# Attention scores for maxima and for exponentials: one ring of four PSUM banks in place of two and two

## The chip, the cores and the metric

The kernel runs on one core of a Trainium2 chip. The metric is the device time of one execution in microseconds (us). A core has engines with instruction queues of their own: TensorE (PE in the profile, with its weight loads as PEld), VectorE (DVE), ScalarE (ACT), GpSimd (POOL) and SyncE (SP), which here only issues transfers. Each queue is worked off in its order; an instruction that waits holds up those behind it on its engine. A matmul writes into PSUM, of which a core has eight banks of 128 partitions by 512 float32 numbers; DVE and ACT read the result from there, and the bank can be written again once it has been read.

## The reference, cut to what matters

The input x has 4 sequences of 512 tokens with 128 features. Four layers follow one another, each added to x after a layer norm: a block with a state-space scan (Mamba) and a mixture of experts, a feed-forward layer, an attention layer, and the same feed-forward layer again. The change is in the attention.

```python
x = x + _L0_attn_a_ref(_layernorm(x), ...)       # scan over 512 tokens, then 8 experts, top 2
x = x + _L0_ffn_ref(_layernorm(x), ...)
x = x + _L0_attn_b_ref(_layernorm(x), ...)       # attention, 16 heads of 8 features
x = x + _L0_ffn_ref(_layernorm(x), ...)
...
q_lat = jnp.einsum('bqhd,hdl->bhql', q, k_eff)
attn = jnp.einsum('bhql,bkl->bhqk', q_lat, c_kv) / sqrt(hs)
attn = jnp.where(causal, attn, -jnp.inf)
attn = jax.nn.softmax(attn, axis=-1)
y_lat = jnp.einsum('bhqk,bkl->bhql', attn, c_kv)
```

The weights of the attention are scaled so that scores are large: the softmax must subtract each row's maximum.

## The kernel before

The first part of the kernel (its last scan step begins at 356.6 us) is the scan, in which the order of the instructions on each engine is written out by hand (`manual_schedule`). The experts, the feed-forward layers and the attention of a sequence follow as soon as its data are there. In the attention's part, from line 1114 on, the order on each engine is not that of the text: a scheduler takes at each step the earliest instruction of the text that could run by its own estimate, and a PSUM or SBUF tile is given a free buffer at that moment. The order that comes out is fixed when the kernel is built; on the chip each engine follows it and waits on semaphores.

The attention works in units: a unit `u` is half the heads (8) of one sequence, so there are 8 units, 0 to 7. For each unit:

- `fill(u)` loads the queries and keys of the unit into the stacks `qs` and `ks` (three of each, taken in turn) from the DRAM tensors `q_d` and `k_d`, with transfers that SP issues. `project(b)` has written these for sequence `b`: layer norm on DVE, `axn` on ACT, transposes and the matmuls `pq` and `pu` on PE, a split into three bfloat16 parts on ACT and POOL, and a transfer to DRAM.
- `maxima(u)` computes all scores with queries on the partitions, 22 bank-sized tiles `sc` a unit: matmuls at line 1186, the causal mask added by a matmul at line 1190, and then a DVE reduction to the row's maximum (`mx`, lines 1182 and 1199). The maxima are split into parts, transposed (`pmx`, line 1209), copied by ACT (`mT`) and written by three transfers that ACT issues (line 1215) into three further rows of `qs`. With them a second matmul of queries and keys yields scores from which the maximum is already subtracted.
- `exps(G)` computes the scores again, with keys on the partitions, for a group `G` of four heads (two groups to a unit, 16 in all): 10 tiles `st` a group, matmuls at line 1238, mask at line 1246, and an ACT exponential of the bank into a tile `p` (line 1251). There are 12 buffers for `p` (`PBUFS`).
- `weigh(G)` multiplies the 10 `p` tiles of a group by the values (`po`, 32 matmul records at line 1265, given a high priority), copies the sum by ACT (`ayT`), transposes it (`pyt`), copies it (`yt`), divides by the sums on DVE and, after the fourth group of a sequence, adds the result to x. The last feed-forward layer of that sequence follows.

The text runs a step of `exps(G)`, one or two steps of `maxima(u + 1)` and a step of `weigh(G - 1)` in turn, and beside them the feed-forward layers and projections of later sequences (`streams`).

Of the eight PSUM banks one is `ps_m` (transposes, projections, `pmx`, `pyt`), two are `ps_s` (feed-forward and experts), one is `ps_o` (`po`). The other four are the subject here:

```python
ps_q, ps_t = pool("ps_q", 2, space=PSUM), pool("ps_t", 2, space=PSUM)   # line 1124
sc = ps_q.tile([P, L], F32, tag="sq", name="sc")                        # line 1183, maxima
pt = ps_t.tile([P, L], F32, tag="st", name="st")                        # line 1234, exps
```

The pools have `reuse_waits="tile"`: the first matmul into a buffer waits for the tile that had the buffer before it, and for no other.

Of the kernel before, what the change touches and what calls it, by code (L numbers as in the profile page):

```python
# [8 lines left out]
F32 = mybir.dt.float32  # L9
# [5 lines left out]
PSUM = bass.MemoryType.PSUM  # L15

P = 128
B, L, C = 4, 512, 128
# [19 lines left out]
def block_kernel(ctx, tc, x, rms1_w, rms2_w, in_proj_w, conv_w, conv_b, x_proj_w,  # L38
# [1075 lines left out]
    with ExitStack() as second:  # L1114
        def pool(name, bufs, **more):
            return second.enter_context(
                tc.tile_pool(name=name, bufs=bufs, reuse_waits="tile", **more)
            )
# [2 lines left out]
        dram = second.enter_context(  # L1121
            tc.tile_pool(name="a_dram", bufs=2, space=bass.MemoryType.DRAM)
        )
        ps_q, ps_t = pool("ps_q", 2, space=PSUM), pool("ps_t", 2, space=PSUM)
        ps_o = pool("ps_o", 1, space=PSUM)


# [93 lines left out]
        def exps(G):  # L1221


            u, h0 = G // 2, 4 * (G % 2)
            q, k = qs[u % 3], ks[u % 3]
            probs[G] = got = [{} for _ in range(4)]

            for blocks in (
                [(0, 0, 0)], [(1, 0, 0)], [(2, 0, 0)], [(3, 0, 0)],
                [(0, 1, 0), (0, 3, L - P)], [(1, 1, 0), (1, 3, L - P)],  # L1230
                [(2, 1, 0), (2, 3, L - P)], [(3, 1, 0), (3, 3, L - P)],
                [(0, 2, 0), (1, 2, 2 * P)], [(2, 2, 0), (3, 2, 2 * P)],
            ):
                pt = ps_t.tile([P, L], F32, tag="st", name="st")
                p = w2.tile([P, L], F32, tag="p", name="p", bufs=PBUFS)
                for j, kt, c in blocks:
                    rows = slice(kt * P, (kt + 1) * P)
                    nc.tensor.matmul(  # L1238
                        pt[:, c : c + L - kt * P], k[:, h0 + j, rows],
                        q[:, h0 + j, kt * P : L],  # L1240
                        start=(c == 0), stop=False, skip_group_check=True,
                    )
                    got[j][kt] = p[:, c : c + L - kt * P]

                n, step = len(blocks), blocks[-1][2] // P or 1
                nc.tensor.matmul(  # L1246
                    pt.rearrange("p (a c) -> p a c", c=P)[:, 0 : step * (n - 1) + 1 : step, :],
                    identb, maskk.unsqueeze(1).to_broadcast([P, n, P]),
                    start=False, stop=True, skip_group_check=True,
                )  # L1250
                ready[G] = nc.scalar.activation(p, pt, AF.Exp, scale=scale).ins  # L1251
                yield
# [82 lines left out]
        for G in range(2 * UNITS + 1):  # L1335
            u = G // 2
            if G % 2 == 0:
# [6 lines left out]
                while u + 1 < UNITS and filled <= u + 1:  # L1344
                    turn(*streams)
                    if filled // 2 in stores:
                        fill(filled)
                        filled += 1
                more = maxima(u + 1) if u + 1 < UNITS else iter(())
            scores = exps(G) if G < 2 * UNITS else iter(())  # L1350
            weighed = weigh(G - 1) if 1 <= G else iter(())
            for step in range(10):
# [74 lines left out]
```

## Time and profile before

| what | value |
|---|---|
| time, median of 3 runs | 882.34 us (880.51 to 889.71) |
| the profiled execution's own time | 900.44 us |
| its span (first to last instruction) | 898.7 us |
| mean granted TensorE clock | 0.904 |
| PE, DVE, ACT, POOL busy | 723.7, 569.0, 409.5, 308.2 us |
| first and last matmul of the maxima (line 1186) | 473.6 and 833.8 us |
| first and last matmul of the exponentials (line 1238) | 523.9 and 871.7 us |
| DVE reductions of maxima, lines 1182 and 1199 | 168 and 8 |
| ACT exponentials, line 1251 | 160, mean 601 ns |

A group of instructions is shown with its source line, engine and operation, the tile written and those read, the count, the busy time and the mean of one, and then how long the engine stood idle before these instructions and what ended most of that. A row of a time stretch gives the busy time of PE, weight loads, DVE, ACT and POOL, the granted clock and the share of the DMA engines. A row of the waits gives who waited for whom: total in us, number of times, longest. The profiled execution was 2.1% longer than the median of the runs.

### The profile page before, as it was taken

What the parts mean: (1) busy time and instruction counts of PE and PEld (TensorE: products, weight loads), DVE (VectorE), ACT (ScalarE), POOL (GpSimd) and SP (SyncE); (2) the same over time, 40 slices, a digit from 0 to 9 for tenths busy, and PEclk for the clock granted to TensorE, in tenths of its full rate; (3) what the DMA queues carried; (4) which work ended last, traced back from release to release, by engine and by line L of the source; (5) the groups of instructions that cost most, each with busy time, mean ns of one, the idle gap of its engine ahead of it and who ended that gap; (6) DMA issues with size and microseconds to landing.
All of it is one profiled execution on the core that took longest, in us unless ns stands there. A gap on an engine that the chain in (4) does not pass through costs nothing.

```text
span 898.7 us, 12363 instructions
## 1 busy us (share of the span) xinstructions
PE 723.7 (81%) x3957; PEld 439.7 (49%) x3967; DVE 569.0 (63%) x1165; ACT 409.5 (46%) x796; POOL 308.2 (34%) x234
## 2 busy tenths in 40 slices
PE   8988797689698986777837789989667897599887
PEld 5633242233276751574724567856433453255445
DVE  4799999889988999563417753337643277166324
ACT  3848655737843541242410245444146533544652
POOL 1155765775675367673122003000331301200000
PEclk9998798879989997888977999999869899889999
DMA  5157221221466644263544437853200310300000
GB/s 134 38 208 284 69 60 42 72 66 49 133 204 193 195 149 119 83 190 124 181 132 135 151 95 218 231 150 113 83 24 1 109 45 3 113 30 13 2 13 12
DMA packets 83258, 95.85 MB, mean 107 GB/s; under 512 B 9841, under 2 KB 56121, under 8 KB 82041
## 3 DMA queue, kind: packets, MB, share of 16 engines
q1 hardware_dynamic: 78681, 87.09, 31.4%
q0 software_dynamic: 2944, 7.34, 2.4%
q10 hardware_dynamic: 1568, 0.63, 0.3%
q8 instruction: 32, 0.52, 0.2%
q14 instruction: 33, 0.27, 0.1%
HBM read 76.47 MB, written 18.28 MB: 105 GB/s over the span
## 4 chain that ended last, share of the span: by engine, by line
PE 28%; DMA 8%; DVE 7%; ACT 6%; issue 5%; POOL 3%; another core or an unknown queue 1%; SPq 1%; ACTq 0%; POOLq 0%; DVEq 0%
PE po L1265 4%; DMA ks<-k_d 4%; PE mpg L380 3%; PE mpd L392 3%; PE mpu L380 3%; ACT p L1251 3%; PE sc L1186 2%; DVE mx L1182 2%; PE pg L451 2%; PE pu L453 2%; PE st L1238 2%; PE fpd L478 2%; DMA wgu<-in_Wg_dram 2%; DMA k_d<-parts 2%
## 5 line engine op out<-in xcount | busy, mean ns | idle before, releaser
L953 POOL TENSOR_TENSOR hc<-hst,cs 128x1024 f32<-128x1024 f32 x63 | 148.3, 2354 | 111.6 <-issue 24.6
L894 PE MATMUL yp<-hc,ident 128*128 128x512 f32 x256 | 145.7, 698 | 41.0 <-POOL hc L953 39.2
L939 DVE TENSOR_TENSOR_SCAN hst<-da,bx 128x1024 f32<-128x1024 f32 x64 | 146.3, 2287 | 9.2 <-POOL hc L953 1.7
L1182 DVE TENSOR_REDUCE mx<-sc 128x1 f32<-128x384 f32 (+3 forms) x168 | 101.8, 635 | 67.6 <-PE sc L1190 66.2
L1251 ACT ACTIVATE p<-st 128x512 f32<-128x512 f32 x160 | 90.6, 601 | 51.5 <-PE st L1246 28.5
L894 PEld LDWEIGHTS yp<-hc,ident 128*128 128x128 f32 x256 | 52.1, 217 | 121.3 <-POOL hc L953 78.7
L1186 PE MATMUL sc<-ks,qs 125*128 125x128 bf16 (+3 forms) x256 | 68.5, 325 | 40.3 <-DMA ks<-k_d 17.6
L874 ACT ACTIVATE da<-delta,A 128x512 f32<-128x512 f32 (+1 forms) x128 | 84.8, 714 | 34.8 <-DVE hst L939 30.0
L323 DVE SCALAR_TENSOR_TENSOR thm<-thm,mpg 128x512 f32<-128x512 f32 x53 | 36.1, 681 | 73.2 <-ACT thm L386 72.5
L916 DVE TENSOR_TENSOR bx<-du,pb 128x1024 f32<-128x1024 f32 x64 | 78.3, 1223 | 6.6 <-PE pb L884 4.7
L415 POOL DMA_INDIRECT yk<-yg,rows_y x32 | 32.3, 1009 | 126.0 <-DMA yg<-ym 82.3
L1238 PE MATMUL st<-qs,ks 128*128 128x384 bf16 (+3 forms) x246 | 58.5, 307 | 20.7 <-ACT p L1251 12.0
L380 PE MATMUL mpg<-xTm,wgu 128*128 128x128 f32 x424 | 64.8, 291 | 6.7 <-DVE thm L323 3.1
L380 PEld LDWEIGHTS mpg<-xTm,wgu 128*128 128x128 f32 x424 | 57.6, 204 | 18.3 <-issue 8.5
L392 PE MATMUL mpd<-wd,mh 128*128 128x128 f32 x424 | 60.2, 286 | 6.0 <-ACT xTm L373 4.3
L380 PE MATMUL mpu<-xTm,wgu 128*128 128x128 f32 x424 | 59.7, 284 | 1.5 <-DVE mh L324 1.4
L392 PEld LDWEIGHTS mpd<-wd,mh 128*128 128x128 f32 x424 | 53.8, 198 | 11.0 <-ACT xTm L373 7.3
L386 ACT ACTIVATE thm<-mpg 128x512 f32<-128x512 f32 x53 | 31.7, 598 | 56.7 <-DVE base L408 32.5
L380 PEld LDWEIGHTS mpu<-xTm,wgu 128*128 128x128 f32 x424 | 54.9, 201 | 2.0 <-DVE mh L324 1.6
L373 ACT ACTIVATE xTm<-mpt,r2w 128x128 f32<-128x128 f32 x53 | 19.4, 366 | 63.2 <-PE mpt L371 55.3
L396 ACT COPY ym<-mpd 128x128 f32<-128x128 f32 x53 | 14.1, 267 | 72.3 <-PE mpd L392 46.0
L1186 PEld LDWEIGHTS <-qs 125*128 125x128 bf16 x256 | 25.4, 106 | 43.7 <-issue 36.0
(261 smaller groups left out, 1202.7 us busy)
## 6 DMA issues: line engine op xcount, KB each, us to landing
cs<-c_d SPq DMA_DIRECT2D x64, 256.0 KB
wgu<-in_Wg_dram SPq DMA_DIRECT2D x53, 256.0 KB
wgu<-in_Wu_dram SPq DMA_DIRECT2D x53, 256.0 KB
wd<-in_Wd_dram SPq DMA_DIRECT2D x53, 256.0 KB
xg<-zero SPq DMA_DIRECT2D x8, 1024.0 KB
qs<-q_d SPq DMA_DIRECT2D x24, 192.0 KB
ks<-k_d SPq DMA_DIRECT2D x24, 192.0 KB
xt<-xg SPq DMA_DIRECT2D x53, 64.0 KB
```

The source lines that it names most:

```text
L323: nc.vector.scalar_tensor_tensor(th, th, 1.0, g, ALU.add, ALU.mult)
L380: nc.tensor.matmul(pp[:, f, :], w[:, k, f * P : (f + 1) * P], rows_in, start=True, stop=True,)
L392: nc.tensor.matmul(pd, hT[:, f, :], w[:, f, :], start=(f == 0), stop=(f == NFC - 1))
L874: nc.scalar.activation(da[:, e, e:], delta[b][:, e, e:], AF.Exp, scale=A[:, e, n : n + 1])
L894: nc.tensor.matmul(yps[b][:, e, :], ident, hc[:, e, :], start=(n == 0), stop=(n == NS - 1))
L916: nc.vector.tensor_tensor(bxs[s], du[s // NS], taps[s][1].unsqueeze(1).to_broadcast([P, NE, L]), ALU.mult)
L939: nc.vector.tensor_tensor_scan(hst.rearrange("p e l -> p (e l)"), dec.pop(s).rearrange("p e l -> p (e l)"), bxs.pop(s).rearrange("p e l -> ...
L953: done = (nc.vector if end else nc.gpsimd).tensor_tensor(hc, hst, cs.unsqueeze(1).to_broadcast([P, NE, L]), ALU.mult).ins
L1182: nc.vector.tensor_reduce(*taken, AX.X, ALU.max)
L1186: nc.tensor.matmul(sc[:, c : c + w], q[0:MXR, h, t * P : w], k[0:MXR, h, 0:w], start=(h == h0), stop=False, skip_group_check=True,)
L1238: nc.tensor.matmul(pt[:, c : c + L - kt * P], k[:, h0 + j, rows], q[:, h0 + j, kt * P : L], start=(c == 0), stop=False, skip_group_check=True,
L1251: ready[G] = nc.scalar.activation(p, pt, AF.Exp, scale=scale).ins
```

## The change

The two pools become one of four banks, and the tiles `st` take the tag of the tiles `sc`. Both kinds of score tile then draw from the same four banks: a tile of either kind takes the next one that is free. No instruction of work is added or removed.

```diff
@@ -1121,7 +1121,8 @@
-        ps_q, ps_t = pool("ps_q", 2, space=PSUM), pool("ps_t", 2, space=PSUM)
+
+        ps_q = ps_t = pool("ps_q", 4, space=PSUM)
         ps_o = pool("ps_o", 1, space=PSUM)
@@ -1231,7 +1232,7 @@
-                pt = ps_t.tile([P, L], F32, tag="st", name="st")
+                pt = ps_t.tile([P, L], F32, tag="sq", name="st")
                 p = w2.tile([P, L], F32, tag="p", name="p", bufs=PBUFS)
```

## The prediction

> **What bounds the kernel now.** The change touches nothing ahead of the first maxima at 473.6 us, so I read the attention's part alone: first the busy time of each engine in stretches, then the waits of PE for its score banks, then the queues of PE, DVE and ACT in order of time where such waits lie. The stretches:
>
> ```profile
> core 0: us, PE busy (x) PEld busy (x) DVE busy (x) ACT busy (x) POOL busy (x), PEclk, DMA share, GB/s
> ...
> 722.00:740.00 18.00, 17.73 (x112) 11.25 (x115) 15.68 (x27) 7.76 (x14) 1.00 (x1) 0.96 0.08 30
> 740.00:758.00 18.00, 14.21 (x97) 7.22 (x90) 16.60 (x50) 3.64 (x8) 0.28 (x1) 0.91 0.01 2
> 758.00:786.00 28.00, 16.56 (x112) 8.31 (x111) 5.13 (x30) 17.47 (x35) 8.70 (x9) 0.86 0.30 90
> 786.00:836.00 50.00, 47.42 (x346) 27.22 (x352) 33.48 (x72) 24.29 (x43) 2.54 (x2) 0.91 0.06 20
> 836.00:877.00 41.00, 34.19 (x264) 17.54 (x256) 7.90 (x27) 24.34 (x48) 1.27 (x1) 0.96 0.03 8
> ```
>
> From 722 to 740 and from 786 to 836 PE is the bound (17.7 of 18, 47.4 of 50 us). From 740 to 758 it is DVE (16.6 of 18): the maxima of unit 5, and between their reductions the layer norm of the last sequence's projection. From 758 to 786 no engine is: the kernel waits for that projection's way through POOL and DRAM (queries and keys of unit 6 land at about 785). From 836 to 877 PE and ACT take turns on the last groups. Before 653 the experts share PE, and from 653 to 722 the end is set by the third sequence's chain of gathers, feed-forward, projection and transfers. The waits for a bank, over 470 to 898 us:
>
> ```profile
> PE st L1238 <- ACT p L1251: 12.0, 16, 3.4
> PE sc L1186 <- DVE mx L1182: 10.7, 38, 0.8
> ```
>
> That is 22.7 us in 54 waits, all that more banks could remove.
>
> **What the change removes.** With four banks behind either kind, a kind that is alone can have four tiles open, not two. PE then gets ahead by two tiles more, once; after that it goes at the reader's pace again. So a run of waits shrinks by two reader steps at most, and only if the reader itself wasn't the bound.
>
> Maxima alone, 740 to 758. PE (time, us, line, idle before) and below it DVE:
>
> ```profile
> 754.48 0.38 PE L1186 MATMUL sc<-ks,qs 125*128 125x512 bf16 x1 [0.25 <-DVE mx L1182]
> ...
> 756.91 0.38 PE L1186 MATMUL sc<-ks,qs 125*128 125x512 bf16 x1 [0.18 <-DVE mx L1182]
> 757.12 0.22 PE L1190 MATMUL sc<-maskq,identb 128*128 128x128 bf16 x1
> 757.18 1.07 PE L539 MATMUL pq<-axT,w_qk 128*128 128x512 f32 x2
> ```
>
> ```profile
> 753.73 3.72 DVE L1182 TENSOR_REDUCE mx<-sc 128x1 f32<-128x512 f32 x6 [0.27 <-PE sc L1190]
> ```
>
> Six reductions stand without a gap in 3.72 us, 0.61 each: DVE sets the pace, and the maxima end when they ended. But `pq`, a step of the last projection, stands behind five such `sc` tiles; its input `axT` was there at 754.2 (ACT 753.62 plus 0.59), and it began at 757.18. Two tiles of lead take 2 x 0.61 = **1.2 us** from it, and `pq` lies on the way to unit 6's keys, for which PE stands idle before 786. This counts in full.
>
> Beside each other, 786 to 836. PE is the bound; 1.2 us of `sc` waits (5 times) lie in it and no `st` wait. At most **1.2 us** go.
>
> Exponentials alone, 836 to 877. PE waits 4.4 us for ACT there, the longest one first (PE), then what ACT did (ACT), then the end of the stretch (ACT, PE):
>
> ```profile
> 844.65 0.38 PE L1238 MATMUL st<-qs,ks 128*128 128x256 bf16 x2 [1.96 <-ACT p L1251]
> ```
>
> ```profile
> 844.00 1.09 ACT L1251 ACTIVATE p<-st 128x512 f32<-128x512 f32 x2 [1.85 <-DMA qs<-mT]
> ...
> 868.41 4.28 ACT L1251 ACTIVATE p<-st 128x512 f32<-128x512 f32 x7
> ```
>
> ```profile
> 872.75 2.36 PE L1265 MATMUL po<-p,va 128*32 128x512 f32 x32 [0.69 <-ACT p L1251]
> ```
>
> At 844 ACT had been issuing the three `mT` transfers (1.96 us from 841.70) and then worked without a gap to the `po` at 847.4, which needs its last exponential: PE's 1.96 us there are covered by ACT, and the gain is nothing. At the end ACT does seven exponentials in 4.28 us, 0.61 each, and the last `po` waits for them. Just before, ACT stood idle for 2.01 and 1.87 us (before `ayT` at 864.04 and `fo` at 866.50) while PE did `po` and `fpd`. The buffers `p` come free with that `po`, at about 864; with two more tiles ready in PSUM, ACT does two exponentials during `fpd`: 2 x 0.61 = **1.2 us** less at the end.
>
> Elsewhere: in 473 to 487 the maxima of unit 0 are paced by DVE (11.9 of 14 us busy, and what is missing is the start): nothing. In 653 to 722 the longest `st` wait (3.4 us at 663.35) has the transpose of `xn` behind it, but `xn` came from ACT at 663.24 to 664.9, late by DVE's layer norm: nothing. Waits before 653 lie beside the experts' transfers: nothing.
>
> Sum of what goes: 1.2 + 1.2 + 1.2 = **3.6 us**.
>
> **What it adds.** No instruction is new. New are two waits: an `sc` tile can now stand behind an exponential, an `st` tile behind a reduction. A group may hold its banks for longer: exponentials run two tiles into the next group (12 `p` buffers, 10 used) and then wait for `po`. Today those that wait hold two banks, with the change up to four, and after `po` a maxima tile must wait for ACT's first exponential, 0.60 us by its row. Behind that `sc` on PE stands whatever follows: feed-forward matmuls, the next `st`. From below: nothing, if the tile behind `po` is not an `sc`, or a bank is free. From above: 0.6 us at each of the two `po` inside the stretch bound by PE (804.70, 816.99), 1.2 us. I take the middle, **+0.6**, since of the two one is followed by an `sc` straight after its mask (807.06), the other by the value matmuls.
>
> The order on the engines is made anew. In the stretches where PE is the bound it picks by place in the text, as today; I give it nothing, and keep plus or minus 6 us for the range: five 0.6 us tiles ahead of `pq` today, as many more or fewer, at two such places.
>
> Sum: -3.6 + 0.6 = **-3.0 us** of the profiled 900.44 us, 0.33%. The runs' median is 0.98 of the profiled time, so -2.9 from 882.34: **879.4 us**.
>
> **Two rules against the rows.** The Trainium skill (Perfetto Trace Analysis, Optimization Strategy) reads the same gap repeating on the engine that should be saturated as a sign that PSUM may have too few buffers. The gaps of 0.16 to 0.25 us ahead of each `sc` are just that. By the rule all 22.7 us would be for the taking, 860 us. Against it speaks another sentence of the skill (TensorE: Matmul & The Clock Gate, HAM oscillation): in a kernel made contiguous, double-buffering PSUM "gave no further gain", which here would mean 882. The row decides: DVE's six reductions without a gap say that the pace isn't PE's, and leave only what stands behind the queue, 3.0 us.
>
> **Rivals.** (1) *Every bank wait from 722 us on counts.* There the end is set by PE or by what stands in its queue: 2.8 + 0.7 (740 to 758) + 2.6 + 1.2 + 4.4 = 11.7 us, and 0.9 of `po` waits: -12.6, scaled **870**. For it: PE is the busiest engine. Against: two of the five terms are covered by DVE or ACT, as shown. (2) *Exponentials that wait for `p` hold all four banks.* The maxima then stand for `po` (2.36 us, as today) and for four exponentials more, 4 x 0.58 = 2.3 us. Four such `po` from 786 to 836 (786.30, 804.70, 816.99, 835.79) cost 9.2 us, two before (712.98, 739.78) 4.6; unit 7's maxima have a slack of 4.0 us (split ready at 836.24, `pmx` on PE at 840.32). Sum +9.8, **892**. It decides from the second such `po` on, when the slack is used up. For it: `st` of a step comes before `sc` in the text. Against: from 743 to 757 the maxima run a unit ahead of the exponentials, so few wait when groups change. (3) *The banks go round in the order of the text.* Then unit 5's maxima couldn't fill the 14 us from 743 to 757 in which unit 4's exponentials aren't allowed yet: up to +14, **896**. Against: PE's queue isn't in the order of the text even now. (4) *Nothing moves*: wherever both kinds run, PE is the bound, and the order stays: **882**.
>
> **Numbers.** My forecast 0.42 (its own range 872 to 888), rival 1 0.20, rival 2 0.22, rival 3 0.08, rival 4 0.08. Faster or slower by 1% (8.8 us, about what a measurement of this kernel can tell from no change): faster is rival 1 and a little of mine, 0.22; slower is rivals 2 and 3 and the order's upper end, 0.31; within 1% the rest, 0.47. The range: 866 to 900 leaves out the lower end of rival 1 and the upper ends of 2 and 3.
>
> **What would show it.** Right: `st` waits for ACT fall from 12.0 to under 7 us and `sc` waits for DVE stay above 6, since DVE paces them; ACT's last run of exponentials is five, not seven; `pq` of the last sequence begins nearer to its `axT` than 3 us. Rival 2: PE waits of `sc` for `p` of over 1 us behind each `po`, DVE idle longer before `mx`. Rival 3: no run of 22 `sc` without an `st`. Wrong altogether: a shift of over 6 us in when the last keys land (785) that comes from the order on POOL, ACT or SP and not from a bank.

## The result: 0.8% slower, and the profile after

| kernel | median | runs |
|---|---|---|
| before | 886.12 us (880.51 to 892.18) | 20 |
| after | 892.14 us (886.73 to 899.48) | 20 |

The ratio is 1.0079, 95% interval [1.0054, 1.0104]. The forecast was 0.33% less, so it had the wrong sign; the time lies in the range. The profiled execution of the kernel after took 892.26 us, close to its median, with a span of 890.5 us and a clock of 0.902. (From line 1125 on its line numbers are one higher than before.)

The waits for a score bank did go. These are the waits of the kernel after (engine, line, waited for, us in total, times, longest), over 460 to 898 us; the first line is not a bank's and is read below:

```profile
PE pt L178 <- ACT xn L167: 19.3, 4, 16.9
...
PE st L1239 <- DVE mx L1183: 1.9, 3, 1.1
PE st L1239 <- ACT p L1252: 1.8, 7, 0.5
...
PE sc L1187 <- ACT p L1252: 1.2, 3, 0.7
...
PE sc L1187 <- DVE mx L1183: 0.9, 5, 0.2
```

In place of 22.7 us in 54 waits there are 5.8 us in 18, and the kernel is slower all the same. New is the first line: one wait of 16.9 us for `xn`, the input of a feed-forward layer. To see where it stands, the stretches of the kernel after (busy us of PE, weight loads, DVE, ACT, POOL; granted clock; DMA share; GB/s):

```profile
600.00:653.00 53.00, 32.34 (x278) 24.63 (x275) 23.89 (x64) 16.90 (x35) 13.24 (x14) 0.83 0.32 94
653.00:690.00 37.00, 31.61 (x220) 18.35 (x220) 26.05 (x103) 20.68 (x40) 4.67 (x5) 0.92 0.02 6
...
740.00:758.00 18.00, 13.68 (x77) 6.89 (x77) 4.64 (x23) 7.84 (x16) 2.92 (x3) 0.72 0.01 2
758.00:786.00 28.00, 23.68 (x174) 12.62 (x173) 15.53 (x49) 16.07 (x31) 5.71 (x6) 0.87 0.30 96
786.00:836.00 50.00, 45.51 (x355) 27.57 (x356) 32.14 (x73) 25.83 (x47) 2.53 (x2) 0.94 0.06 17
```

The execution of the kernel before that the prediction used was 14 us over its own median. For the comparison I take the control of the first experiment instead: the kernel before with its own order written down (ratio to before 1.0005). Its two first stretches:

```profile
600.00:653.00 53.00, 41.22 (x273) 27.91 (x272) 32.10 (x86) 16.93 (x36) 16.25 (x17) 0.81 0.25 76
653.00:690.00 37.00, 29.68 (x172) 14.53 (x171) 12.79 (x73) 21.91 (x44) 9.09 (x10) 0.90 0.12 34
```

From 600 to 653 PE does 32.3 us of work where it did 41.2, and DVE 23.9 where it did 32.1. The work has moved into the next stretch: DVE 26.1 us there in place of 12.8. The tiles say which work it is. The 22 maxima tiles of unit 3 were reduced from 604.9 to 642.1 us in the control; in the kernel after they are reduced from 657.7 to 683.4. The first and the last line of these reductions, in the control and then in the kernel after:

```profile
604.91 1.28 DVE L1182 TENSOR_REDUCE mx<-sc 128x4 f32<-128x512 f32 x2
...
641.43 0.68 DVE L1199 TENSOR_REDUCE mx<-sc 128x1 f32<-128x512 f32 x1
```

```profile
657.65 2.58 DVE L1183 TENSOR_REDUCE mx<-sc 128x4 f32<-128x512 f32 x4
...
682.70 0.69 DVE L1200 TENSOR_REDUCE mx<-sc 128x1 f32<-128x512 f32 x1
```

**Why they moved.** PE's queue holds 176 maxima tiles (m) and 160 exponential tiles (E). Their order from the start of the attention, before and after:

```
before  m x44  E x24  mm EE mm E m E m E m E m E mmm EE m E m E mm E m ...  m x25  E x30 ...
after   m x22  E m E mm E m E mm ... E m  E x6  m E mm E m E mm ... (so to the end)
```

After is the order of the text: one exponential, then one or two maxima, and six exponentials where a unit ends. In both orders no tile stands ahead of an earlier one of its own tag. Two tiles of one tag are handed out by this scheduler in the order in which the text asks for them, so a tile can't be given a bank ahead of one that stands before it in the text. With two tags that held inside each kind, and the maxima could run a whole unit ahead of exponentials that weren't due yet. With one tag it holds across both kinds. The sentence in the description of the kernel that a tile is given a free buffer when its instruction is taken is true between tags only. The change thus did two things: it made four banks of two and two, and it tied the two kinds' order.

### The profile page after: what moved, and what is told of

The parts are those of the page before. It is cut to its first block, busy times and chain, and to the rows that moved or that the text cites. A ratio compares the mean times of both kernels' runs of the same rounds, so it can differ in the third digit from the quotient of the medians.

```text
span 890.5 us, 12376 instructions
## 1 busy us (share of the span) xinstructions
PE 712.7 (80%) x3967; PEld 443.8 (50%) x3967; DVE 569.2 (64%) x1165; ACT 411.3 (46%) x796; POOL 307.4 (35%) x234
## 3 DMA queue, kind: packets, MB, share of 16 engines
q1 hardware_dynamic: 78681, 87.09, 32.1%
## 5 line engine op out<-in xcount | busy, mean ns | idle before, releaser
L953 POOL TENSOR_TENSOR hc<-hst,cs 128x1024 f32<-128x1024 f32 x63 | 149.0, 2366 | 110.3 <-issue 23.5
L894 PE MATMUL yp<-hc,ident 128*128 128x512 f32 x256 | 143.2, 687 | 42.5 <-POOL hc L953 40.4
L1183 DVE TENSOR_REDUCE mx<-sc 128x1 f32<-128x384 f32 (+3 forms) x168 | 98.6, 634 | 87.7 <-PE sc L1191 87.4
L1187 PE MATMUL sc<-ks,qs 125*128 125x128 bf16 (+3 forms) x256 | 66.5, 330 | 24.7 <-DMA ks<-k_d 14.3
L380 PE MATMUL mpg<-xTm,wgu 128*128 128x128 f32 x424 | 65.5, 295 | 14.6 <-DVE thm L323 7.3
L1239 PE MATMUL st<-qs,ks 128*128 128x512 bf16 (+3 forms) x256 | 62.8, 312 | 7.7 <-DMA qs<-mT 3.6
L380 PE MATMUL mpu<-xTm,wgu 128*128 128x128 f32 x424 | 62.1, 291 | 0.0
L380 PEld LDWEIGHTS mpu<-xTm,wgu 128*128 128x128 f32 x424 | 57.5, 208 | 0.0
L1191 PE MATMUL sc<-maskq,identb 128*128 128x128 bf16 (+2 forms) x176 | 47.4, 269 | 0.0
```

Of the source, the lines that this page charges most:

```text
L380: nc.tensor.matmul(pp[:, f, :], w[:, k, f * P : (f + 1) * P], rows_in, start=True, stop=True,)
L894: nc.tensor.matmul(yps[b][:, e, :], ident, hc[:, e, :], start=(n == 0), stop=(n == NS - 1))
L953: done = (nc.vector if end else nc.gpsimd).tensor_tensor(hc, hst, cs.unsqueeze(1).to_broadcast([P, NE, L]), ALU.mult).ins
L1183: nc.vector.tensor_reduce(*taken, AX.X, ALU.max)
L1187: nc.tensor.matmul(sc[:, c : c + w], q[0:MXR, h, t * P : w], k[0:MXR, h, 0:w], start=(h == h0), stop=False, skip_group_check=True,)
L1191: nc.tensor.matmul(sc[:, 0 : n * w].rearrange("p (h k) -> p h k", k=w)[:, :, t * P : w], identb, maskq.unsqueeze(1).to_broadcast([P, n, P] ...
```

## The experiments

Every kernel was compared with runs of the kernel before on the same chip. One table of stretches serves them all, in us of one profiled execution each: from the first reduction of the maxima on DVE to the first gather of the experts' rows for sequences 2 and 3 (a), to the feed-forward layer's first transpose for sequence 2 (b), to project's store of `k_d` for sequence 2 (c), the same for sequence 3 (d), and to the end of the span (e). The ratio is that of all its runs to before.

| kernel | a | b | c | d | e | ratio and interval |
|---|---|---|---|---|---|---|
| two_old_order | 165.5 | 19.3 | 39.4 | 66.1 | 129.7 | 1.0005 [0.9983, 1.0027] |
| two_new_order | 170.1 | 18.0 | 50.7 | 66.0 | 130.2 | 1.0127 [1.0089, 1.0166] |
| after | 171.9 | 18.1 | 48.6 | 63.6 | 124.4 | 1.0079 [1.0054, 1.0104] |
| lock_early | 172.5 | 18.1 | 47.7 | 65.5 | 128.1 | 1.0174 [1.0132, 1.0215] |
| lock_late | 168.1 | 19.2 | 39.1 | 61.8 | 127.2 | 0.9918 [0.9879, 0.9957] |
| lock_unit2 | 165.7 | 18.1 | 46.3 | 64.1 | 129.6 | 1.0034 [1.0016, 1.0052] |
| lock_units01 | 171.6 | 21.5 | 37.6 | 63.2 | 128.3 | 1.0104 [1.0067, 1.0142] |
| lock_units013 | 171.0 | 21.6 | 39.0 | 68.6 | 128.2 | 1.0049 [1.0028, 1.0069] |
| four_late | 166.6 | 19.2 | 39.2 | 60.5 | 124.5 | 0.9874 [0.9821, 0.9927] |
| four_ahead | 160.6 | 26.3 | 41.7 | 81.1 | 119.5 | 1.0158 [1.0122, 1.0194] |
| ahead_012 | 164.5 | 29.1 | 44.2 | 58.9 | 123.0 | 0.9969 [0.9951, 0.9987] |
| ahead_02 | 168.7 | 26.0 | 41.8 | 59.3 | 124.3 | 0.9925 [0.9902, 0.9949] |
| ahead_2 | 168.7 | 23.5 | 41.8 | 58.9 | 122.8 | 0.9946 [0.9923, 0.9970] |

One execution strays by some us from its median, so the table shows where a kernel loses; how much it loses is read from the ratio. How far a stretch strays is seen from the first profile of the kernel before, the same program as two_old_order: it has 165.2, 24.1, 39.1, 65.7 and 130.0 us. Between these two b differs by 4.8 us, the others by 0.4 at most.

### Order or banks

Two kernels keep two banks for each kind. One has the queues of PE, DVE, ACT and SP tied to the order of the kernel before, the other to that of the kernel after (POOL's order is the same in both). The edit, for both:

```diff
+ORDERS = {
...
+def in_order(tc, names, engines):
...
+        for a, b in zip(row, row[1:]):
+            tc.add_manual_dep(b, a.name, order, reason="the order written down")
...
         block_kernel(tc, *args)
+        in_order(tc, ORDERS, ('PE', 'DVE', 'Activation', 'SP'))
```

two_old_order, the control:

> The kernel before, with each engine's queue (PE, DVE, ACT, SP) written down in the order that it has anyway. Any theory: the same program, ratio 1.000 within 0.3%. It gives a second profile of the kernel before, whose first one was 14 us longer than its median: I expect a span near 885 us, the first maxima at 460 to 466 us.

two_new_order:

> Two banks for each kind as before, but each engine's queue (PE, DVE, ACT, SP) in the order of the changed kernel, in which score tiles follow the text: no maxima tile ahead of an exponential's tile that stands before it in the text. Theory A (the order is the cost, the banks themselves give a little back): slower than before by 0.8 to 1.3%, 893 to 898 us, at or above the changed kernel's 892. Theory B (the shared banks cost, by tiles that hold a bank the other kind needs; the order is neutral): 884 to 888 us, ratio 0.998 to 1.002.

Measured: 1.0005 and 1.0127. The order alone, with no bank changed, makes the kernel slower by 1.3%; writing an order down costs nothing. In the table the loss stands in a (4.6 us) and c (11.3 us). In a the experts' last matmul comes 166.4 us after the first reduction of maxima where it came after 161.6; why it does I haven't traced, and what follows explains c. What the banks give back is after against two_new_order, the same queues with four banks: 1.0079 against 1.0127, about 0.5% or 4 us, though the two intervals overlap. In the profiles most of it lies in e, 130.2 against 124.4 us, and there the table divides by the banks: the eight profiles with two banks for each kind at the end have 127.2 to 130.2 us, that of the kernel before among them, the six with four have 119.5 to 124.5. The reverse, four banks in the old order, can't be had: inside one tag the old order isn't possible. It wasn't tried.

### Early units or late ones

Here only the first matmul of each score tile is tied to the one before it in the text, in chosen units; all other instructions are ordered by the scheduler as before.

```diff
+        def in_text_order(ins, where):
+            if not (where < 4):            # lock_early; lock_late: where >= 4
+                tied.clear()
+                return
+            if tied:
+                tc.add_manual_dep(ins, tied[0].name, order, reason="score tiles in the order of the text")
+            tied[:] = [ins]
...
+                        if h == h0:
+                            in_text_order(ins, u - 1)                 # maxima(u)
...
+                    if (j, kt, c) == blocks[0]:
+                        in_text_order(ins, u)                         # exps, unit u
```

> Two banks for each kind as before; score tiles are tied to the order of the text for the exponentials of units 0 to 3 and the maxima of units 1 to 4, and free after that. Theory A, with the loss where the two first profiles show it (first maxima to the third sequence's keys in DRAM, 229 us before and 240 after): slower by 0.8 to 1.5%, 893 to 899 us. If the loss lies in the later units: within 0.3% of before. Theory B: within 0.3% of before.

> Two banks for each kind as before; score tiles are tied to the order of the text only for the exponentials of units 4 to 7 and the maxima of units 5 to 7. Theory A, with the profiles read as above (196 us from there to the end before, 188 after): faster than before by 0.4 to 0.9%, 878 to 883 us. If the loss lies in the later units: slower by 0.8 to 1.5%. Theory B: within 0.3% of before.

Measured: 1.0174, more than the 0.8 to 1.5% expected, and 0.9918. Together they make 0.9%, by the intervals no contradiction to the 1.3% of the whole order. The same tie loses in the first half and gains in the second: the order isn't bad in itself, its place decides. The late gain can be read line by line in the layer norm of the last sequence's projection. In two_old_order these are the input `x`, the norm's first and last step on DVE, the transposed result `axT`, the last `sc` tile ahead of `pq`, and `pq` itself, for which the norm is wanted:

```profile
723.09 1.27 POOL L484 TENSOR_TENSOR x<-base,fo 128x512 f32<-128x512 f32 x1 [19.89 <-ACT fo L483]
...
724.40 0.87 DVE L153 BATCH_NORM_STATS2 st<-x 128x6 f32<-128x128 f32 x4 [0.46 <-POOL x L484]
...
732.06 0.15 DVE L162 SCALAR_TENSOR_TENSOR nm<-mv,rs_r 128x4 f32<-128x4 f32 x1
...
737.72 0.59 ACT L182 COPY axT<-pt 128x512 f32<-128x512 f32 x1 [3.50 <-PE pt L178]
...
741.05 0.38 PE L1186 MATMUL sc<-ks,qs 125*128 125x512 bf16 x1 [0.19 <-DVE mx L1182]
...
741.32 1.07 PE L539 MATMUL pq<-axT,w_qk 128*128 128x512 f32 x2
```

In lock_late, where no `sc` stands ahead of `pq`:

```profile
725.07 1.27 POOL L484 TENSOR_TENSOR x<-base,fo 128x512 f32<-128x512 f32 x1 [19.76 <-ACT fo L483]
...
726.38 0.87 DVE L153 BATCH_NORM_STATS2 st<-x 128x6 f32<-128x128 f32 x4 [0.46 <-POOL x L484]
...
730.65 0.16 DVE L162 SCALAR_TENSOR_TENSOR nm<-mv,rs_r 128x4 f32<-128x4 f32 x1
...
733.47 0.58 ACT L182 COPY axT<-pt 128x512 f32<-128x512 f32 x1 [0.52 <-PE pt L178]
...
734.11 1.22 PE L539 MATMUL pq<-axT,w_qk 128*128 128x512 f32 x1 [0.77 <-ACT axT L182]
```

From the start of `x` to `pq` it is 18.2 us in the one and 9.0 in the other. The norm takes 7.8 us from first to last step where unit 5's reductions stand between its steps, 4.4 where they don't; then the transposes and `pq` stand between and behind the `sc` tiles of unit 5 on PE, or don't: from the norm's last step to `pq` it is 9.3 us in the one and 3.5 in the other. In the early half the exchange goes the other way. In two_old_order the norm of sequence 2's projection runs from 666.47 to 670.96, 4.5 us, since unit 3's maxima are long done; in the kernel after they stand between its steps, and it takes 7.6. First and last step in two_old_order, then the kernel after:

```profile
666.47 0.87 DVE L153 BATCH_NORM_STATS2 st<-x 128x6 f32<-128x128 f32 x4 [4.61 <-POOL x L484]
...
670.83 0.13 DVE L162 SCALAR_TENSOR_TENSOR nm<-mv,rs_r 128x4 f32<-128x4 f32 x1
```

```profile
677.65 0.87 DVE L153 BATCH_NORM_STATS2 st<-x 128x6 f32<-128x128 f32 x4 [0.65 <-POOL x L484]
...
678.72 0.66 DVE L1183 TENSOR_REDUCE mx<-sc 128x1 f32<-128x512 f32 x1
679.29 0.16 DVE L428 TENSOR_SCALAR ln_v<-mv 128x4 f32<-128x4 f32 x1
679.36 0.68 DVE L1183 TENSOR_REDUCE mx<-sc 128x1 f32<-128x512 f32 x1
...
679.96 0.16 DVE L136 TENSOR_SCALAR rs_t<-ln_v 128x4 int32<-128x4 int32 x1
...
685.10 0.14 DVE L162 SCALAR_TENSOR_TENSOR nm<-mv,rs_r 128x4 f32<-128x4 f32 x1
```

In the rows from 679.29 to 682.63 each small step (0.16 us) waits for a reduction of 0.68. These 3.1 us are a third of the 9.2 by which stretch c grew; another 4.6 lie ahead of it, in the feed-forward layer, which shares PE with the same maxima: from its first transpose to `x` it takes 22.4 us (653.90 to 676.34) against 17.8 (647.37 to 665.17). And while these maxima could have run (the last transfer of their queries and keys was issued at 590.3 us), PE stood idle, since the transpose of `xn` is next in its queue (kernel after, PE; in two_new_order, with two banks for each kind, the same wait takes 17.5 us):

```profile
635.06 1.93 PE L1146 MATMUL pv<-veff,qk 64*128 64x128 f32 x8 [0.66 <-ACT mT L1214]
653.90 0.47 PE L178 MATMUL pt<-ident,xn 128*128 128x128 f32 x1 [16.91 <-ACT xn L167]
```

### Which early unit

The same tie as above, with other conditions:

```diff
-            if not (where < 4):
+            if not (where == 2):           # lock_unit2
+            if not (where < 2):            # lock_units01
+            if not (where in (0, 1, 3)):   # lock_units013
```

> Two banks for each kind, as before; only the score tiles of unit 2's exponentials and unit 3's maxima are tied to the order of the text, so that the 22 tiles of unit 3's maxima no longer run in one piece ahead of unit 2's exponentials. Theory A (most of the early loss is that unit 3's maxima move from the stretch at 605 to 641 us, where PE waits for the experts and the gathers, to a place beside ffn and project of sequence 2): the way from the transposes of ffn's xn to project's store of k for sequence 2 grows by 7 to 10 us over the 39.4 us of the two banks with their own order, and the time is 0.7 to 1.2% above before, 891 to 895 us. Rival C (the loss is spread over the early units alike, since each tied tile waits for its neighbour): about a quarter of the 1.7% of the four tied units, 0.4%, 888 to 889 us. Rival D (the loss comes from the end of the experts, which units 0 and 1 delay): within 0.3% of before.

> Two banks for each kind; tied are only the exponentials of units 0 and 1 and the maxima of units 1 and 2. Theory A: the first gathers of the experts' rows come 4 to 8 us later than the 628 us of the two banks with their own order, unit 3's maxima stay ahead of the gathers, the way through ffn and project of sequence 2 keeps its 39 to 41 us, and the time is 0.3 to 0.8% above before, 888 to 892 us. Rival C (spread alike): two quarters of 1.7%, 0.8 to 0.9%, 892 to 893 us. Rival D (all of the loss sits here): 1.4 to 1.7%, 897 to 900 us.

> Two banks for each kind; tied to the order of the text are the score tiles of lock_early (exponentials of units 0 to 3, maxima of units 1 to 4) without those of unit 2's exponentials and unit 3's maxima. Theory G (unit 2's tie is dear when its neighbours are tied too: with four banks its release alone took the time from 1.0079 to 0.9946): most of lock_early's 1.7% goes, 1.003 to 1.008 of before. Theory H (the shares of the units add up: 1.74% less lock_unit2's 0.34%): 1.012 to 1.016.

Measured: 1.0034, 1.0104 and 1.0049. Lock_unit2 stretches c by 6.9 us to 46.3, nearly what theory A expected, but the time rises by 0.3% only, as rival C said; in its profile 1.2 us come back in b and 2.0 in d. Lock_units01 delays the gathers by 6 us, as A expected, and costs 1.0%, more than A's 0.3 to 0.8% and again nearest to C. So by these two the loss seemed spread alike. But then lock_units013, three of the four units, should cost some 1.3%; it costs 0.5% and fits theory G: without unit 2's tie most of lock_early's 1.7% is gone, and c is back at 39.0 us. So unit 2's tie is worth 1.25% beside the others and 0.3% by itself. The parts don't add up, and one pair is odd: lock_units013 ties more than lock_units01 and costs no more, by intervals that just touch. How the early loss divides among the units stays open; that it is an early loss, and that taking unit 2's tie away recovers most of it, does not.

### Four banks without the early loss

First, two and two banks up to unit 3, and four from there:

```diff
-        ps_q, ps_t = pool("ps_q", 2, space=PSUM), pool("ps_t", 2, space=PSUM)
+        ps_q, ps_t, tag = scores_from("ps_q", 2), scores_from("ps_t", 2), "st"
...
             u = G // 2
+            if G == 8:
+                banks.close()
+                ps_q = ps_t = scores_from("ps_qt", 4)
+                tag = "sq"
```

> Two banks for each kind up to unit 3's exponentials and unit 4's maxima, and from there on four banks that both kinds take in turn. Theory A (order and banks add up: the late order alone measured 0.9918, and the banks gave back 0.5% where the order was held): 0.986 to 0.992 of before, 873 to 878 us; the waits of late score tiles for a bank fall under 2 us. Rival E (the banks' gain came in the early units, or goes when the pools are exchanged in mid-course, where the new tiles wait for all old ones): 0.992 to 0.998, 878 to 883 us.

Measured: 0.9874, as theory A had it. It is faster than both kernels (876.6 us against 883.87 of before on that chip), and 0.4% better than lock_late, with overlapping intervals again. The two share the order of the score tiles, but not of everything: some transposes, feed-forward matmuls and exponentials stand elsewhere in the queues of PE, DVE and ACT. As in the pair after and two_new_order, e is where the banks show, 127.2 against 124.5 us. The bank waits of late tiles (710 to 876 us) are 1.2 us, all of `st` for ACT, so under 2 as expected; but lock_late had only 2.3 there, 1.2 of `st` and 1.1 of `sc`. What went is 1.1 us, less than the 4 us between the two ratios.

Then the other way, with one tag throughout: if the text sets the order, change the text.

```diff
                 more = maxima(u + 1) if u + 1 < UNITS else iter(())
+                for _ in range(22 if u < 4 else 0):        # four_ahead
+                    next(more)
```

> Four banks in turn, as in the changed kernel, but the text has all 22 tiles of the next unit's maxima ahead of the exponentials of units 0 to 3, and from unit 4 on it is the changed kernel's text. Theory A (the loss is the order that one tag forces, and the text sets that order): unit 3's maxima run again before the gathers, at 600 to 645 us, the way through ffn and project of sequence 2 falls from the changed kernel's 49 us to 39 to 43, and the time is 0.985 to 0.995 of before, 872 to 880 us. Rival F (sharing the banks itself costs in the early units, whatever the order, for instance because maxima that wait for the fill hold a bank that exponentials would have had): still 1.002 to 1.010 of before, 887 to 894 us.

Measured: 1.0158, far from theory A's number and past rival F's as well. Unit 3's maxima do run before the gathers, and stretches a, c and e are good; b is 7 us longer than in the control, and most of the loss is in d, 81.1 us. Its cause stands in one line of PE (four_ahead):

```profile
683.28 2.07 PE L549 MATMUL pu<-qk,w_up 64*128 64x512 f32 x2 [1.16 <-ACT full L553]
708.37 0.58 PE L1187 MATMUL sc<-ks,qs 125*128 125x128 bf16 x4 [23.03 <-DMA ks<-k_d]
```

My edit had put unit 4's maxima ahead of unit 3's exponentials too. Unit 4 is the first of sequence 2, whose keys were only being stored; with one tag the exponentials, ready all the time, stand behind them, and PE has nothing for 23.0 us. So the next runs leave that unit out:

```diff
-                for _ in range(22 if u < 4 else 0):
+                for _ in range(22 if u < 3 else 0):        # ahead_012
+                for _ in range(22 if u in (0, 2) else 0):  # ahead_02
+                for _ in range(22 if u == 2 else 0):       # ahead_2
```

> Four banks in turn; the text has all 22 tiles of the next unit's maxima ahead of the exponentials of units 0, 1 and 2 (four_ahead without unit 3). Theory A2 (four_ahead lost because unit 3's exponentials stood behind unit 4's maxima, which waited 23.0 us for sequence 2's stored k): that wait goes, and the stretch from project's store of k for sequence 2 to that of sequence 3 falls from 81 us to 63 to 68; the time falls by 10 to 15 us from four_ahead's, to 0.995 to 1.005 of before, and if nothing else is out of place to 0.985 to 0.995. Rival F (sharing the banks costs in the early units whatever the order): 1.005 to 1.012.

> Four banks in turn; the maxima of units 1 and 3 stand whole ahead of the exponentials of units 0 and 2, those of the other units as in the changed kernel. It is the text that comes nearest to the order in which the kernel before runs its score tiles up to unit 3. Theory A2: first gathers 165 to 168 us after the first maxima, the way from ffn's transposes to project's store of k for sequence 2 39 to 43 us, and 0.986 to 0.995 of before, 872 to 880 us. Rival F: 1.003 to 1.010.

> Four banks in turn; only unit 3's maxima are put whole ahead of the exponentials of unit 2. Theory A2: by lock_unit2's 0.3% the time falls from the changed kernel's 1.008 to 1.003 to 1.006 of before, since units 0 and 1 keep the order that cost 1.0% in lock_units01. Rival D (unit 3's maxima carry the whole early loss): 0.986 to 0.994.

Measured: 0.9969, 0.9925 and 0.9946. With unit 4 left out d falls from 81.1 to 58.9 us, further than the 63 to 68 that I expected. Ahead_02 is within its numbers (a just above). Ahead_2 differs from the changed kernel by one loop, which moves 22 tiles in the text, and takes it from 1.0079 to 0.9946: 1.3% for the place of unit 3's maxima, more than I expected and just past the upper end of rival D's range. Rival F, that sharing the banks itself costs in the early units, is out: all four banks are shared in all three. None reaches four_late; in each of them b is 4 to 10 us longer than there, of which some 5 us can be the straying of b. In ahead_02 a part is the same kind of wait, on ACT: `xn` could be made when its norm ends on DVE (first row), and stands 5 us behind the copy and the transfers of unit 3's maxima:

```profile
658.73 0.16 DVE L162 SCALAR_TENSOR_TENSOR nm<-mv,rs_r 128x4 f32<-128x4 f32 x1
...
661.41 0.57 ACT L1214 COPY mT<-pmx 24x512 bf16<-24x512 bf16 x1 [6.54 <-remote]
...
662.01 1.95 ACTq L1216 DMA_DIRECT2D qs<-mT  x3
664.01 1.65 ACT L167 ACTIVATE xn<-base,nm,rs_r 128x128 f32<-128x128 f32 x4 [1.54 <-DMA qs<-mT]
```

In ahead_012 and ahead_2 `xn` follows its norm at once, so b is longer there for another reason, which I haven't traced.

## Why the prediction was wrong

**The failed step** is this one: "The order on the engines is made anew. In the stretches where PE is the bound it picks by place in the text, as today; I give it nothing". The order was worth +1.27% (two_new_order), some 11 us, against the 6 us that I kept for it in the range; and I looked for it at two places of the late units. It lost early, at a place that the sum had closed with "Waits before 653 lie beside the experts' transfers: nothing". That spoke of the waits and not of the work: the maxima of unit 3 used PE and DVE in those pauses, and couldn't any more.

**Rival 3 was the mechanism**, at 0.08. I put it aside because "PE's queue isn't in the order of the text even now". That is no argument: with two tags the queue is free between the kinds whatever the rule inside one. Its place was wrong as well. In the 14 us of unit 5's maxima, where I priced it at +14, the tie is a gain: lock_late, which ties exactly the late units, is at 0.9918, since those maxima stood in front of the last projection.

**The banks' part** agrees in sign and size as far as the runs tell. Forecast: -3.0 us. Measured by two pairs: about 0.5% (two_new_order to after, all queues the same) and 0.4% (lock_late to four_late, the score tiles in the same order), some 4 us each, neither pair with separate intervals. This bears out the sum, not its terms: none of the three gains of 1.2 us was measured by itself, and the signs below that belong to two of them came from the order. Rival 1 (-12.6 us) and the first of the two rules of the Trainium skill in the prediction (all 22.7 us of the repeating gaps, 860) are far from this: in the new order 13 us of bank waits, 18.9 in two_new_order less 5.8, brought about 4. Of the two rules the second, that double-buffering gave no further gain, was nearer. The waits of the same queues with two banks (two_new_order, 460 to 898 us):

```profile
PE sc L1186 <- DVE mx L1182: 10.3, 27, 1.9
PE st L1238 <- ACT p L1251: 8.6, 16, 2.7
```

**The signs I had named.** `st` waits for ACT under 7 us: 1.8, and with two banks in the same order 8.6, so this one is the banks'. `sc` waits above 6 us: 0.9, wrong. I had thought of runs of maxima alone that DVE paces, and after unit 0 there is none left; from 740 to 758, where DVE was the bound with 16.6 of 18 us, it is busy for 4.64. `pq` near its `axT`: 748.85 against 748.79, and five exponentials at the end in place of seven: five. Both look like hits and are none, because two_new_order has them too, with two banks (753.76 against 753.70; five): the order of the queues brought them. For the five it is ACT's queue: lock_late, with the score tiles of the end in the order of the text, still has seven there, four_late five. These are the lines of the kernel after:

```profile
748.21 0.58 ACT L182 COPY axT<-pt 128x512 f32<-128x512 f32 x1 [2.07 <-DMA qs<-mT]
748.85 2.08 PE L539 MATMUL pq<-axT,w_qk 128*128 128x512 f32 x2 [2.00 <-ACT axT L182]
...
861.87 2.63 ACT L1252 ACTIVATE p<-st 128x512 f32<-128x512 f32 x5
864.55 2.36 PE L1266 MATMUL po<-p,va 128*32 128x512 f32 x32 [1.47 <-ACT p L1252]
```

Rival 2's sign, `sc` waits for `p` of over 1 us behind each `po`, isn't there: 1.2 us in 3 waits, the longest 0.7. That its 892 us is the measured time is chance. Rival 3's sign is there: after unit 0 no more than two `sc` follow one another without an `st`. "Wrong altogether: a shift of over 6 us in when the last keys land" did come true. Sequence 3's `k_d` is stored 302.2 us after the first reduction of maxima, against 290.3 in two_old_order (a to d summed). I had named POOL, ACT and SP; the rows show it on PE and DVE. POOL's order is the same before and after; those of ACT and SP changed too, and no run holds their part apart.

## What to carry to other kernels

Two kinds of tile that take their buffers from one ring are, with a scheduler that hands out a ring in the order of the text, also tied in their order: the one that is early in the text holds back the other, however long its own data take. Before two rings are joined, ask which kind runs ahead of the other today, where it does so, and which pauses it fills there; if that is worth keeping, order the text so first or join the rings only where the order doesn't matter. And work that is off the critical path has a place all the same: price where it goes, not only the waits that go.

## What I had not expected

A layer norm of small DVE steps (0.16 us each) stretches from 4.4 or 4.5 to 7.6 or 7.8 us when reductions of 0.68 us stand between them in DVE's queue, and this decided both the early loss and the late gain in part. And the time depends on the chip by more than the change moved it: the kernel before had a median of 883.87 us on one and of 897.41 us on another, so each kernel was set against runs of the kernel before on its own chip.
